# A graph layer on one core: edge loads after the first thirteen move from SyncE's queue to GpSimd's

## The chip, the cores and the metric

The kernel runs on one core of one Trainium2 chip. The metric is the device time of one execution in microseconds, with fp32 data throughout. A core has five engines with a queue of instructions each: TensorE (matrix products), VectorE (called DVE in the profile), ScalarE (ACT), GpSimd (POOL) and SyncE (SP). Any of SP, ACT and POOL can issue DMA transfers; all transfers of the core run on its 16 DMA engines.

## What is computed

The reference is one layer of a graph network, cut here to what matters:

```python
h   = relu(layernorm(x))                       # x: 12500 x 128
agg = segment_sum(edge_attr_48, dst, 12500)    # edge_attr: 412500 x 48, dst sorted
u   = graph_globals[0]                         # 64 numbers, the same for all nodes
hid = relu(concat([h, agg, u]) @ W1 + b1)      # W1: 240 x 256
out = x + (hid @ W2 + b2)                      # W2: 256 x 128
```

Each edge's 48 features are added into the row of its destination node; `dst` is sorted, so neighbouring edges go to neighbouring nodes. Then comes a small two-layer perceptron for each node. The edges are 79 MB of the 95 MB that are moved.

## The kernel before, in words

**The sum over edges as matrix products.** Edges are cut into 403 chunks of 1024 (128 partitions x 8). A chunk is split into two halves of the work, `s = 0` (chunks 0 to 200) and `s = 1` (201 to 402), that go through the kernel side by side. Six chunks make a group; there are 34 groups in each half. For a group, VectorE builds a one-hot matrix (`onehot`, L317): for every edge, 44 columns that compare its shifted destination with 0 to 43. TensorE multiplies the edge features with it (`contract`, L327) and gathers 48 x 199 sums in PSUM. `add` (L343) adds these into `aggT` at the column where the group begins.

**The loop.** The order is written out by hand (the scheduler takes the program's order). The main loop (L647) makes 207 steps; step `CG*i + k` contracts chunk `k` of group `i` of both halves. The rest of the work is placed at steps: a planner dictionary (`at_step`) for dst blocks, `next_x` for loads of x, `next_part` for the layer norm, and a list `pieces` for the perceptron with costs and a credit per step (L666 to 669).

**Edge tiles.** An edge tile `e` holds two chunks, so one load is 384 KB, 128 partitions by two rows of 1536 B. The pool has `PF = 13` buffers. `e_loads` lists the loads in the order in which chunks are used. `next_edges` (L164) takes the next one, allocates a tile and calls `load_edges` (L142). Thirteen are called before the loop (L249); after that each call comes from `contract` (L333), when the last chunk of a tile has been multiplied. The load then has to wait until TensorE has really finished with the buffer.

**Queues.** Before the change SyncE issues: three small loads of `first`, all edge loads (L146), the loads of dst blocks 1 and later (L175, L179; block 1 after the seventh edge load, L252), and all stores of the output (L536, after `ot` has been computed by VectorE, L533). ScalarE issues the loads of x (L211) and dst block 0. GpSimd issues the eight loads of weights (L287 to 294), after its memsets; in the loop it has only two memsets, `mid` (L642) and the pad of the last, short edge tile (L150), whose two remaining loads (L151, L154) are SyncE's.

**The start.** dst block 0 covers two groups, block 1 the next nine. For each block, `shift_dst` (L372) subtracts the base, `spread` transposes it on TensorE (L393) and copies it to `rel`, from which the one-hots are built.

**The perceptron.** For each block of 512 nodes: layer norm (L465, L451, L461), transposes (L477), first layer (L495 for h, L506 for agg, L514 for the relu), second layer (L525) and the sum with x (L533).

Of the kernel before, what the change touches and what calls it, by code (L numbers as in the profile page):

```python
# [21 lines left out]
def kernel(  # L22
# [30 lines left out]
    nc = tc.nc  # L53
# [17 lines left out]
    NFULL = E // CE  # L71
# [67 lines left out]
    bad = const.tile([1, 1], I32)  # L139


    def load_edges(e, c0, n):  # L142

        f = min(n, NFULL - c0)
        if f:
            nc.sync.dma_start(  # L146
                e[:, :f], edge_attr[c0 * CE:(c0 + f) * CE].rearrange("(c p t) d -> p c (t d)", p=P, t=T))
        if f < n:
            last = TAIL // T
            nc.gpsimd.memset(e[:, f], 0.0)  # L150
            nc.sync.dma_start(  # L151
                e[:last, f], edge_attr[NFULL * CE:NFULL * CE + last * T].rearrange("(p t) d -> p (t d)", t=T))
            if TAIL % T:
                nc.sync.dma_start(  # L154
                    e[last:last + 1, f, :(TAIL % T) * DE],
                    edge_attr[None, NFULL * CE + last * T:E].rearrange("a t d -> a (t d)"))

    edges, hots, rels = {}, {}, {}

    e_loads = sorted(  # L160
# [3 lines left out]
    def next_edges():  # L164
        if e_loads:
            _, s, c, n = e_loads.pop(0)
            e = ep.tile([P, CL, T * DE], F32, name="e")
            load_edges(e, c, n)
            for k in range(n):
                edges[c + k] = (e[:, k], k == n - 1)  # L170

    def load_chunks(di, at, c, n, queue):

        full = max(0, min(n, NFULL - c))
        queue.dma_start(di[at:at + full], dst[c * CE:(c + full) * CE].rearrange("(c e) -> c e", e=CE))  # L175
        if full < n:
            for q in range(0, CE, TAIL):
                m = min(TAIL, CE - q)
                queue.dma_start(di[at + full:at + n, q:q + m], dst[None, E - m:E])  # L179
# [57 lines left out]
    with nc.allow_non_contiguous_dma(reason="a few hundred numbers, once"):  # L237
        for s in range(2):
            mid0 = C0[s] * CE
            n = min(NI, (E - mid0) // GE)  # L240
# [8 lines left out]
    for i in range(PF):  # L249
        next_edges()  # L250
        if i == 6:
            dis[1] = load_dst(1, nc.sync)  # L252
# [40 lines left out]
        nc.gpsimd.dma_start(w2, W2.rearrange("(a p) d -> p a d", p=P))  # L293
        nc.gpsimd.dma_start(b2_sb, b2[None, :].to_broadcast([P, D]))

    step = -4
    for k in range(XBUFS):
        load_x(k)
    warm = const.tile([P, 1], F32)
# [20 lines left out]
    def contract(i, k):  # L320

        ps = acc[i % len(acc)]
        o = OFF[k] - OFF[0]
        groups = [(s, s * NI + i, C0[s] + i * CG + k) for s in range(2) if k < chunks[s * NI + i]]
        for t in range(T):
            for s, g, c in groups:
                nc.tensor.matmul(  # L327
                    ps[s * HI:s * HI + DE, o:o + W], edges[c][0][:, t * DE:(t + 1) * DE],
                    hots[g][:, k * T + t, :], start=(k == 0 and t == 0),
                    stop=(k == chunks[g] - 1 and t == T - 1), skip_group_check=True)  # L330
        for s, g, c in groups:
            if edges.pop(c)[1]:
                next_edges()  # L333
# [55 lines left out]
    def turn_dst(df, rows, t0, pool, name):  # L389
        dv = df.rearrange("c (p t) -> c t p", t=T)  # L390
        pt = pool.tile([P, T // 2, P], F32, name=name)
        for t in range(T // 2):
            nc.tensor.transpose(pt[:, t, :rows], dv[:rows, t0 + t, :], ident[:rows, :rows])  # L393
        return pt[:, :, :rows]
# [284 lines left out]
    with tc.If(isbad >= 1):  # L679
        with tc.tile_pool(name="any", bufs=1) as ap:  # L680
            lo_row = ap.tile([1, P], I32, name="lo_row")
            hi_row = ap.tile([1, P], I32, name="hi_row")
            iota_a = ap.tile([P, WA], F32, name="iota_a")
            nc.gpsimd.iota(iota_a, pattern=[[1, WA]], base=0, channel_multiplier=0,
                           allow_small_or_imprecise_dtypes=True)
            nc.gpsimd.memset(aggT, 0.0)

            def windows(s, e_view, r_view, c):
                low_s, high_s = (0, END - 1) if s == 0 else (END, N - 1)
                lo, hi = [nc.values_load(row[0:1, c], min_val=low_s, max_val=high_s,  # L690
                                         skip_runtime_bounds_check_because="clamped on the chip")
                          for row in (lo_row, hi_row)]
                r = ap.tile([P, T], F32, name="r")
                nc.vector.tensor_scalar(r, r_view, float(WA), None, OP.add)
                with tc.For_i(lo, hi + 1, WA) as at:
                    at = nc.s_assert_within(at, low_s, high_s, skip_runtime_bounds_check_because="at most hi")
                    nc.vector.tensor_scalar(r, r, float(-WA), None, OP.add)
                    oh = ap.tile([P, T, WA], F32, name="oh2")
                    nc.vector.tensor_tensor(oh, iota_a[:, None, :].to_broadcast([P, T, WA]),
                                            r[:, :, None].to_broadcast([P, T, WA]), OP.is_equal)  # L700
                    h = slice(s * HI, s * HI + DE)
                    ps = acc[0][h, :WA]
                    for t in range(T):
                        nc.tensor.matmul(ps, e_view[:, t * DE:(t + 1) * DE], oh[:, t, :],
                                         start=(t == 0), stop=(t == T - 1))
                    to = aggT[h, ds(at + shift[s], WA)]
                    nc.vector.tensor_tensor(to, to, ps, OP.add)


            for s, (low_s, high_s) in enumerate(((0, END - 1), (END, N - 1))):  # L710
                for c0 in range(0, NCH, GB):
                    rows = min(GB, NCH - c0)
                    di = dp.tile([P, CE], I32, name="di", bufs=2)
                    load_chunks(di, 0, c0, rows, nc.sync)
                    df = dp.tile([P, CE], F32, name="df", bufs=2)
                    nc.vector.tensor_copy(df[:rows], di[:rows])
                    ends = ap.tile([P, 2], F32, name="ends")
                    nc.vector.tensor_reduce(ends[:rows, 0:1], df[:rows], AX.X, OP.min)
                    nc.vector.tensor_reduce(ends[:rows, 1:2], df[:rows], AX.X, OP.max)

                    nc.vector.tensor_scalar(ends[:rows], ends[:rows], float(low_s), float(high_s), OP.max, OP.min)
                    nc.vector.tensor_scalar(df[:rows], df[:rows], ends[:rows, 0:1], None, OP.subtract)
                    for q, row in ((0, lo_row), (1, hi_row)):
                        pr = pst.tile([1, P], F32, name="pt")
                        nc.tensor.transpose(pr[:, :rows], ends[:rows, q:q + 1], ident[:rows, :rows])
                        nc.vector.tensor_copy(row[:, :rows], pr[:, :rows])
                    rel = ap.tile([P, P, T], F32, name="rel")
                    for t0 in (0, T // 2):
                        nc.scalar.copy(rel[:, :rows, t0:t0 + T // 2].rearrange("p c t -> p t c"),
                                       turn_dst(df, rows, t0, pst, "pt"))  # L730
                    full = min(rows, NFULL - c0)
                    with tc.For_i(0, full, 1) as c:
                        e = ap.tile([P, T * DE], F32, name="e2")
                        nc.sync.dma_start(
                            e, edge_attr[ds(c * CE + c0 * CE, CE)].rearrange("(p t) d -> p (t d)", t=T))
                        windows(s, e, rel[:, ds(c, 1), :].rearrange("p c t -> p (c t)"), ds(c, 1))
                    if full < rows:
                        e = ap.tile([P, 1, T * DE], F32, name="e3")
                        load_edges(e, NFULL, 1)
                        windows(s, e[:, 0], rel[:, full, :], slice(full, full + 1))  # L740
        for s in range(2):
            copy_middle(s)
# [45 lines left out]
```

## Time and profile before

| what | us |
|---|---|
| median of 3 runs (lowest, highest) | 345.6 (343.14, 347.08) |
| the profiled execution's own time | 343.35 |
| its span in the trace | 341.6 |
| TensorE busy (matmuls) in it | 303.0 |
| VectorE busy | 253.5 |
| ScalarE busy | 110.6 |
| GpSimd busy | 13.1 |

The granted clock of TensorE was 0.975 over the span. DMA moved 95.35 MB, 279 GB/s on average. In the rows of the profile, PE is a matmul, PEld a weight load, and a name with q (SPq) the queue of the engine itself; "x <- y: a, b, c" in a table of waits is a us in total, b times, c us the longest. A row of a timeline has the start, the duration, the engine, the line, the operation and its tiles.

### The profile page before, as it was taken

The numbers are of one execution on the slowest core, as the hardware profiler recorded it, in microseconds if no ns is written. First come the engines' busy times: TensorE is split into PE (matmuls) and PEld (weight loads), VectorE is DVE, ScalarE is ACT, GpSimd is POOL, SyncE is SP. The second block draws the span as 40 slices with busy tenths as digits, with TensorE's granted clock in tenths as the row PEclk, the third lists the DMA queues.
The fourth block names the chain that finished last, engine by engine and source line by source line (L and its number), as shares of the span: only waits on it lengthen the run. The fifth ranks groups of instructions, "written<-read, shape, count | busy, mean of one in ns | idle before, by whom it ended". The sixth has DMA issues, their size and how long they took to land.

```text
span 341.6 us, 17111 instructions
## 1 busy us (share of the span) xinstructions
PE 303.0 (89%) x7787; PEld 241.3 (71%) x7788; DVE 253.5 (74%) x413; ACT 110.6 (32%) x238; POOL 13.1 (4%) x44
## 2 busy tenths in 40 slices
PE   1756887999999999889999999889999999999991
PEld 1745764886886786677797696677796796886561
DVE  3768888699896888758878789778899499872320
ACT  3011751805243240333251451233441441251220
POOL 9500000000000000000000000000000000000000
PEclk9969899999999999989999999999999999999998
DMA  5999999999998999998999888989999999920110
GB/s 164 316 356 373 371 372 317 280 347 313 341 289 285 318 300 301 313 310 277 297 335 309 280 300 280 382 266 347 311 304 324 311 296 318 310 97 3 65 63 23
DMA packets 62812, 95.35 MB, mean 279 GB/s; under 512 B 4385, under 2 KB 55949, under 8 KB 62730
## 3 DMA queue, kind: packets, MB, share of 16 engines
q1 hardware_dynamic: 58864, 87.17, 77.1%
q10 hardware_dynamic: 3578, 6.50, 5.7%
q8 instruction: 63, 1.03, 1.3%
q0 software_dynamic: 288, 0.49, 0.5%
q14 instruction: 19, 0.16, 0.1%
HBM read 87.74 MB, written 6.40 MB: 276 GB/s over the span
## 4 chain that ended last, share of the span: by engine, by line
PE 77%; DVE 10%; issue 4%; DMA 4%; SPq 2%; ACT 1%; DVEq 0%; ACTq 0%
PE ps L327 39%; PE po L525 14%; PE ph L495 12%; PE ph L506 7%; DVE oh L317 5%; PE pt L477 4%; DMA di<-in_dst_dram 4%; DVE st L465 1%; PE pt L393 1%; SPq L146 1%; DVE aggT L343 1%; ACT hid L514 1%; ACT xn L461 0%; SPq L241 0%; ACT sc L451 0%
## 5 line engine op out<-in xcount | busy, mean ns | idle before, releaser
L327 PEld LDWEIGHTS ps<-oh,e 128*48 128x48 f32 x6448 | 174.9, 128 | 56.5 <-issue 48.0
L327 PE MATMUL ps<-oh,e 128*48 128x44 f32 x6448 | 183.3, 220 | 8.2 <-issue 4.8
L317 DVE TENSOR_TENSOR oh<-iota,rel 128x2112 f32<-128x2112 f32 (+2 forms) x72 | 157.3, 2205 | 3.8 <-ACT rel L385 2.9
L525 PE MATMUL po<-w,hid 128*64 128x128 f32 (+1 forms) x784 | 59.7, 281 | 3.1 <-issue 2.3
L514 ACT ACTIVATE hid<-ph,bias 128x512 f32<-128x512 f32 (+1 forms) x50 | 31.1, 673 | 85.0 <-PE ph L506 80.9
L495 PE MATMUL ph<-hT,w1h 128*64 128x512 f32 (+1 forms) x200 | 51.9, 597 | 2.5 <-ACT hid L514 2.5
L343 DVE TENSOR_TENSOR aggT<-aggT,ps 48x199 f32 (+1 forms) x68 | 24.3, 357 | 38.8 <-PE ps L327 21.3
L525 PEld LDWEIGHTS po<-w,hid 128*64 128x64 f32 (+1 forms) x784 | 44.4, 139 | 5.9 <-issue 4.2
L461 ACT ACTIVATE xn<-xt,sh,sc 128x128 f32<-128x128 f32 (+1 forms) x100 | 40.6, 484 | 1.7 <-DVE sh L455 1.4
L533 DVE TENSOR_TENSOR ot<-po,xb 128x512 f32<-128x512 f32 (+1 forms) x25 | 17.3, 691 | 18.1 <-PE po L525 17.7
L480 ACT COPY hT<-pt 128x512 f32<-128x512 f32 (+1 forms) x25 | 14.3, 574 | 48.5 <-PE pt L477 48.3
L506 PE MATMUL ph<-aggT,w1a 48*64 48x512 f32 x192 | 26.5, 615 | 0.0
L477 PE MATMUL pt<-ident,xn 128*128 128x128 f32 (+1 forms) x100 | 18.1, 293 | 6.3 <-issue 3.2
L465 DVE BATCH_NORM_STATS2 st<-xt 128x6 f32<-128x128 f32 (+1 forms) x100 | 22.8, 279 | 0.0
L451 ACT ACTIVATE sc<-va,eps 128x8 f32<-128x8 f32 (+1 forms) x13 | 3.9, 301 | 47.2 <-DVE va L450 47.0
L477 PEld LDWEIGHTS pt<-ident,xn 128*128 128x128 f32 (+1 forms) x100 | 10.8, 142 | 10.2 <-issue 3.8
L491 DVE TENSOR_TENSOR xb<-xt,b_sb 128x512 f32<-128x512 f32 (+1 forms) x25 | 16.3, 682 | 0.0
L495 PEld LDWEIGHTS ph<-hT,w1h 128*64 128x64 f32 x200 | 11.1, 137 | 5.1 <-ACT hid L514 3.5
L385 ACT COPY rel<-pt 128x216 f32<-128x216 f32 (+2 forms) x9 | 4.3, 478 | 28.6 <-PE pt L393 28.6
L393 PE MATMUL pt<-ident,df 108*128 108x108 f32 (+2 forms) x36 | 6.3, 302 | 7.2 <-DVE df L372 7.2
L401 ACT ACTIVATE far<-df,bounds 108x1024 f32<-108x1024 f32 (+2 forms) x10 | 11.5, 1145 | 0.2
L150 POOL MEMSET e<- 128x384 f32 x1 | 0.4, 423 | 284.8 <-PE ps L327 284.8
(77 smaller groups left out, 68.3 us busy)
## 6 DMA issues: line engine op xcount, KB each, us to landing
e<-in_edge_attr_dram SPq DMA_DIRECT2D x200, 384.0 KB
xt<-in_x_dram ACTq DMA_DIRECT2D x24, 256.0 KB
out_dram<-ot SPq DMA_DIRECT2D x24, 256.0 KB
di<-in_dst_dram SPq DMA_DIRECT2D x6, 216.0 KB
e<-in_edge_attr_dram SPq DMA_DIRECT2D x2, 192.0 KB
di<-in_dst_dram SPq DMA_DIRECT2D x2, 108.0 KB
e<-in_edge_attr_dram SPq DMA_DIRECT2D x1, 159.0 KB
w1h<-in_L_gnn_W_dram POOLq DMA_DIRECT2D x1, 128.0 KB, 6.8
```

Source lines behind the costliest of these rows:

```text
L317: nc.vector.tensor_tensor(hots[g][:, k0 * T:(k0 + n) * T], iota[:, None, :].to_broadcast([P, n * T, W]), r[:, :, None].to_broadcast([P, n ...
L327: nc.tensor.matmul(ps[s * HI:s * HI + DE, o:o + W], edges[c][0][:, t * DE:(t + 1) * DE], hots[g][:, k * T + t, :], start=(k == 0 and t == ...
L343: nc.vector.tensor_tensor(to, to, acc[i % len(acc)][h, :wg], OP.add)
L461: nc.scalar.activation(xns[j][:m, r], xs[j][:m, r], AF.Relu, bias=sh[:m, c:c + 1], scale=sc[:m, c:c + 1])
L465: parts.append((k, None, lambda i=i, j=j, r=r: nc.vector.bn_stats(st[:m, i * R + r, :], xs[j][:m, r, :])))
L477: nc.tensor.transpose(pt[:, r, :m], xn[:m, r], ident[:m, :m])
L491: nc.vector.tensor_tensor(xb[:m], xs[j][:m], b2_sb[:m, None, :].to_broadcast([m, R, D]), OP.add)
L495: nc.tensor.matmul(phs[j, a][c:c + HI, :R * m], w1h[:, a * P + c:a * P + c + HI], hTs[j][:, :R * m], start=True, stop=False, skip_group_ch ...
L506: nc.tensor.matmul(phs[j, a][c:c + HI], w1a[h, a * P + c:a * P + c + HI], aggT[h, at:at + BN], start=False, stop=True, skip_group_check=True)
L514: nc.scalar.activation(hids[j][:, a, :, :m], phs.pop((j, a))[:, :R * m].rearrange("h (p r) -> h r p", r=R), AF.Relu, bias=bias[:, a:a + 1])
L525: nc.tensor.matmul(pos[j][c:k, r], hids[j][:, a, r, c:k], w2[:, a], start=(a == 0), stop=(a == NH - 1), skip_group_check=True)
L533: nc.vector.tensor_tensor(ot[:m], pos.pop(j)[:m], xbs.pop(j)[:m], OP.add)
```

## The change

`load_edges` and so `next_edges` name the queue that issues the main part of a load. It is SyncE while `step` is below 0, which holds for the thirteen loads before the loop, and GpSimd after that. For this `step = -4` is set further up. The loads of the short last tile stay with SyncE, and so does the edge load of a branch that is not taken with these inputs (L739).

```diff
-    def load_edges(e, c0, n):
+    def load_edges(e, c0, n, queue):
 
         f = min(n, NFULL - c0)
         if f:
-            nc.sync.dma_start(
+            queue.dma_start(
                 e[:, :f], edge_attr[c0 * CE:(c0 + f) * CE].rearrange("(c p t) d -> p c (t d)", p=P, t=T))
...
+    step = -4
     edges, hots, rels = {}, {}, {}
...
             e = ep.tile([P, CL, T * DE], F32, name="e")
-            load_edges(e, c, n)
+            load_edges(e, c, n, nc.sync if step < 0 else nc.gpsimd)
...
-    step = -4
     for k in range(XBUFS):
         load_x(k)
...
-                        load_edges(e, NFULL, 1)
+                        load_edges(e, NFULL, 1, nc.sync)
```

## The prediction

> **What bounds the kernel now.** I read the page first, then the chain of waits, then the two tables of waits (the engines' and SyncE's own queue), then the stretches around the first 40 us and around the gaps of TensorE, and last GpSimd's timeline.
>
> ```profile
> span 341.6 us, 17111 instructions
> PE 303.0 (89%) x7787; PEld 241.3 (71%) x7788; DVE 253.5 (74%) x413; ACT 110.6 (32%) x238; POOL 13.1 (4%) x44
> ...
> q8 instruction: 63, 1.03, 1.3%
> ...
> PE 77%; DVE 10%; issue 4%; DMA 4%; SPq 2%; ACT 1%; DVEq 0%; ACTq 0%
> ```
>
> TensorE is the bound: 303.0 of 341.6 us busy and 77% of the chain. DVE (10%) and one DMA (4%) own the chain only at the start. GpSimd is empty: 13.1 us, nearly all before 13.4 us. Keep the q8 row in mind: 1.03 MB in 63 packets is 16 KB each, and TensorE's 15,575 instructions over 63 are 247 per packet. So TensorE's own program comes in over the same DMA engines as the edges.
>
> In the engines' waits there is one row in which anybody waits for an edge load; below it are the three rows of TensorE alone between 60 and 300 us:
>
> ```profile
> PEld ps L327 <- DMA e<-in_edge_attr_dram: 2.4, 5, 0.8
> ...
> PE ps L327 <- issue: 3.7, 9, 1.0
> PE pt L477 <- issue: 3.2, 2, 1.7
> PE po L525 <- issue: 2.3, 3, 1.6
> ```
>
> Edges cost TensorE 2.4 us in the whole kernel, 1.0 of it before 60 us. The 9.2 us of "issue" (14 gaps) are larger. The long ones on the chain are at 102.61, 138.15, 148.45, 218.29 and 224.32 us (0.73 + 1.02 + 1.69 + 1.52 + 1.61 = 6.57 us); between 136 and 140 us the DMA view reads 379 GB/s against 279 over the span. My reading is that an instruction block arrived late because the engines were full.
>
> SyncE's queue shows why edges are not late:
>
> ```profile
> SPq L146 <- PE ps L327: 135.6, 143, 2.6
> SPq L536 <- DVE ot L533: 48.2, 17, 13.1
> SPq L146 <- DMA e<-in_edge_attr_dram: 22.0, 19, 2.8
> ```
>
> An edge load (L146) waits for TensorE to give a buffer back, in 143 of its waits. So loading runs a full ring of 13 buffers ahead. 202 loads go out from 3.0 to 297.0 us, 1.46 us apart, and 13 of them are 19 us of reserve. The stores (L536) hold the queue up only for 15.2 us between 60 and 300 us, 3.2 at most, well inside that reserve; the rest of the 48.2 comes when no load is left.
>
> **The change part by part.**
>
> *Issue on SyncE falls away:* 189 loads (202 less 13) by the 0.368 us median of L146 are 70 us of a queue nobody waits for. Worth 0.
>
> *Issue on GpSimd is added.* The rows nearest to it:
>
> ```profile
> 7.33 4.89 DVE L317 TENSOR_TENSOR oh<-iota,rel 128x704 f32<-128x704 f32 x6
> ...
> 11.81 0.76 POOL L293 DMA_DIRECT2D w<-in_L_gnn_W_dram  x1
> 12.55 0.56 POOL L294 DMA_DIRECT2D b_sb<-in_L_gnn_b_dram  x1
> 13.08 0.32 POOL L642 MEMSET mid<- 128x212 f32 x1
> ...
> 298.20 0.42 POOL L150 MEMSET e<- 128x384 f32 x1 [284.81 <-PE ps L327]
> ```
>
> The W2 load has the pattern of an edge load (128 partitions by two rows), so I take its 0.76 us: 189 x 0.76 = 144 us, against the 282 us from 15 to 297 (1.49 us per load). GpSimd is half full and keeps up. What hides this is the 19 us of reserve. Without it, a load would be late by 0.76 - 0.37 = 0.39 us each time (189 x 0.39 = 74 us). Value 0; the bounds are 0 and that 74, and 0 is near because the L146 waits say that the reserve is whole.
>
> *A rule that speaks against it.* The Trainium skill, page "SBUF — State Buffer", section "SBUF: two separate sides", says that for a DMA issued by GpSimd its own cores write the descriptors, through a port pair shared with VectorE; a VectorE operation that holds both ports keeps them out until it ends. Taken at its worst, GpSimd issues nothing during the one-hots (L317, 157.3 us, some 147 of them after 15 us): 144 + 147 = 291 us in a window of 282, a kernel 9 us longer. The trace argues against the worst: six one-hots ran back to back from 7.33 to 12.22 us (0.815 us each) while six of GpSimd's eight DMA issues ran at 0.5 to 0.8 us inside the same stretch; neither had a gap. The same section also counts an operation with two SBUF inputs, which the one-hot is, as in the way only of a GpSimd operation that reads SBUF. I go by the row: 0.
>
> *What is queued behind a waiting GpSimd load:* more edge loads, the memset of `mid` (moves from 13 us to behind the loads of the first twelve steps; first read when 28 of 34 groups are done), and the memset of L150, for which SyncE's two tail loads wait (298.7 us, used by TensorE at 313). No one near the chain. SyncE keeps stores and dst loads, which no longer stand behind edge loads; the only wait for one of them is the 5.0 us of L372 for dst block 1, issued with the first thirteen.
>
> *The start changes.* Today load 14 goes out at 20.8 us, since SyncE sends seven loads, then mostly one each time an older one has landed. GpSimd is not behind these: it is free at 13.4 us, and if it too keeps eight in flight, its first edge load waits for its first weight load to land (8.33 + 6.8 = 15.1 us). Five buffers are free by 15.42 us (TensorE has done five steps), so up to five loads of 384 KB start some 5 us earlier. Nobody waits for them. They share engines with this transfer, which is on the chain:
>
> ```profile
> 7.11 12.49 DMA di<-in_dst_dram
> ```
>
> dst block 1 lands at 19.60 us; DVE waits for it, then the one-hots, then TensorE (idle from 15.42 to 21.00). With another ring beside it from about 16 us, its last 2.6 us (my estimate, from its landing less a microsecond) stretch by at most 3072/4096 of themselves, if edges come in packets of two rows: +2.0. But weights and x already share it until about then: bounds 0 and +2.0, I take +0.7. From 20 to 57 us DVE sets the pace, so nothing gives this back.
>
> *Edge waits:* the 1.4 us after 60 us may vanish, as loads no longer stand behind a store. Bounds 0 and -2.4; I take -1.4.
>
> *Instruction blocks.* The second rule: page "DMA: Bandwidth & Descriptors", section "Queues, rings and completion order", says that an engine takes turns between rings packet by packet. By it a block of instructions waits for about one edge packet; if GpSimd's packets hold two rows, that is 3072 B instead of 1536, at 23 B/ns per engine (375 GB/s over 16) 0.07 us more, 63 x 0.07 = +4 us if nothing hides it. The trace disagrees with the rule's picture of a short wait: the first weight load (128 KB, 8 KB per engine) took 6.8 us to land behind seven edge loads. A newcomer waits for a backlog, whichever ring holds it; then the change is worth nothing here. Bounds -6.6 (the five gaps go) and +4; I go by the row, 0.
>
> *Sum:* -1.4 + 0.7 + 0 = -0.7 us on the profiled execution's 343.35 us (341.6 span and 1.75 around it) gives 342.65. The median of the runs, 345.6, lies 2.25 above that execution, so 344.9 on the median.
>
> **Rivals.**
>
> (A) *The transfer is hidden anyway*, the forecast: 344.9, its own range 342.2 to 348.5. For it: 143 waits for buffers, 19 us of reserve. Chance 0.40.
>
> (B) *GpSimd becomes the bound.* One mechanism, in the loop of loads: if an issue there costs over 1.49 us instead of 0.76, loads fall behind TensorE and the reserve drains. At 291 us of GpSimd time it is +9, so 355. Against it: the overlapped rows above. For it: the trace has only eight such issues, none with a wait in front. Chance 0.14. An off-shoot: the DMA engines are slower on GpSimd's rings. The need is about 310 GB/s and 375 were reached, so over 17% worse would decide; 360 and more, 0.04.
>
> (C) *Contention at the start and at instruction blocks:* +2.0 for dst and +4 for blocks, with no gain: 351.6. For it: PE gaps already coincide with full engines, and x loads on ACT and edges would both be free to run earlier. Chance 0.15.
>
> (D) *The block gaps close*, because loads leave one by one as buffers come free and not in bursts after a blocked queue: -1.4 and -6.6 + 0.7 is -7.3, so 338.3 at best; half of the gaps give 341.6. For it: the gaps fall where the engines are full. Against: TensorE itself frees buffers in bursts. Chance 0.27.
>
> (E) *It does not do what it says:* from GpSimd the loads could still come no earlier, since buffers decide. That is part of A.
>
> **How the numbers follow.** 1% is 3.5 us, about what a measurement of this kernel can tell from no change. A is "within 1%": 0.40. B with its off-shoot and C are slower: 0.33. D is faster: 0.27. The range holds A, D down to 339 and C and B up to 355, leaving out the slow off-shoot and the ends of B and D.
>
> **What would show it.** Right: L146 as a POOL row of about 0.76 us, its waits mostly for PE; PE's "issue" rows still near 9 us; L372's wait for dst near 5 to 7 us; "PEld ps <- DMA e" under 2.4. B: that row at tens of us and POOL's issues above 1.4 us. C: dst landing after 21 us, more and longer issue gaps. D: the five gaps gone and TensorE's busy share above 90%. The forecast falls if loads from GpSimd land much later than a free buffer, or if TensorE's instruction blocks react to whose ring the edges are in.

## The result, and the profile after

| | median us | lowest, highest | ratio to before [95%] |
|---|---|---|---|
| before, beside it | 346.34 | 343.14, 347.48 | 1 |
| changed kernel | 360.66 | 357.85, 364.57 | 1.0402 [1.0281, 1.0522] |
| before, on another chip | 349.18 | 345.83, 351.25 | 1 |
| changed kernel, on that chip (`a2_after`) | 357.69 | 355.78, 360.88 | 1.0239 [1.0186, 1.0292] |

The change costs 2.4 to 4.0%. The forecast was no change (344.9, in a range up to 355). The profiled execution after took 357.85 us, 14.5 more than the one before (343.35). Medians are of all runs; ratios are of the fast ones alone, those within 1.5% of the fastest of their kernel ("none" where there was only one).

The page after: span, busy times, queues, chain, and two groups (busy us and mean ns of one; idle us before them and who ended it).

```profile
span 356.1 us, 17111 instructions
...
PE 308.6 (87%) x7787; PEld 246.3 (69%) x7788; DVE 253.7 (71%) x413; ACT 110.9 (31%) x238; POOL 147.6 (41%) x233
...
q0 software_dynamic: 21408, 74.63, 64.0%
q1 hardware_dynamic: 7584, 13.03, 10.9%
...
PE 76%; DMA 9%; DVE 6%; issue 5%; SPq 1%; ACT 1%; DVEq 0%; ACTq 0%
...
L146 POOL DMA_DIRECT2D e<-in_edge_attr_dram x189 | 134.4, 712 | 164.6 <-PE ps L327 159.1
L317 DVE TENSOR_TENSOR oh<-iota,rel 128x2112 f32<-128x2112 f32 (+2 forms) x72 | 157.4, 2205 | 4.0 <-ACT rel L385 3.2
```

GpSimd issues a load in 0.71 us and for 159.1 of its 164.6 idle us waits for TensorE to free a buffer: it is not the bound. A one-hot of VectorE takes 2205 ns, as before. DMA now has 9% of the chain, against 4%, and almost all of it lies in two pieces (chain in order of time: start, us, what):

```profile
5.93 13.45 DMA e<-in_edge_attr_dram
19.81 17.73 DMA e<-in_edge_attr_dram
```

Both are edge loads of **SyncE**. The first is the seventh; SyncE waited for it to land before it issued the eleventh. The second is the twelfth of the first thirteen, issued at 19.81 us. TensorE needed it, and it landed at 37.54. The engines' waits, then the issues in the whole kernel, then those from 7.5 to 20.6 us alone (last number: median us from issue to landing):

```profile
PEld ps L327 <- DMA e<-in_edge_attr_dram: 14.6, 22, 2.9
PE ps L327 <- DMA e<-in_edge_attr_dram: 7.2, 4, 2.8
...
DVE df L372 <- DMA di<-in_dst_dram: 3.7, 1, 3.7
```
```profile
e<-in_edge_attr_dram POOLq DMA_DIRECT2D x188, 384.0 KB, 5.4
```
```profile
e<-in_edge_attr_dram SPq DMA_DIRECT2D x6, 384.0 KB, 18.8
e<-in_edge_attr_dram POOLq DMA_DIRECT2D x5, 384.0 KB, 9.1
```

Waits for edges were 2.4 us and are 21.8 (14.6 + 7.2). Before 45 us they are 15.0 (7.8 and 7.2). Most of the rest is a label: each of GpSimd's loads landed at least 9 us before the first product that used it. GpSimd's first five edge loads, issued from 15.94 to 19.73 us, took 9.1 us in the median. SyncE's last six were issued from 8.02 to 20.32 us; the trace gives the landing of only one of them, the thirteenth tile, and the 18.8 is that one (39.12 us). By the packets on SyncE's ring the thirteen tiles were complete at 25.2 us before and at 38.2 after. So tiles 14 to 18 were there first, and TensorE waited for tiles 9 to 12 and took the thirteenth as it landed. What the engines carried from 20 to 36 us says why (packets, MB, share of 16 engines), before and then after:

```profile
DMA packets 4006, 5.98 MB, mean 374 GB/s; under 512 B 261, under 2 KB 3620, under 8 KB 4004
...
q1 hardware_dynamic: 3572, 5.16, 91.9%
```
```profile
DMA packets 2472, 5.85 MB, mean 366 GB/s; under 512 B 252, under 2 KB 1365, under 8 KB 2469
...
q0 software_dynamic: 983, 3.47, 59.1%
q1 hardware_dynamic: 1053, 1.55, 28.0%
```

The bytes are nearly the same; their order is not. q1 is SyncE's ring, q0 GpSimd's (a ring is the list of transfers that one queue has handed to the DMA engines). The two rings took about as many turns (983 and 1053 packets), but most of GpSimd's packets hold three rows of 1536 B (15,072 packets of 4608 B in the kernel), SyncE's one. So the loads that were due got 1.55 MB and those that were not got 3.47. TensorE's timeline shows the price (start, us, matmuls, then the idle time before); the last row is from the kernel before:

```profile
25.07 1.51 PE L327 MATMUL ps<-oh,e 128*48 128x44 f32 x30 [0.36 <-DMA e<-in_edge_attr_dram]
28.52 1.67 PE L327 MATMUL ps<-oh,e 128*48 128x44 f32 x34 [1.94 <-DMA e<-in_edge_attr_dram]
32.96 1.51 PE L327 MATMUL ps<-oh,e 128*48 128x44 f32 x30 [2.77 <-DMA e<-in_edge_attr_dram]
...
37.58 4.37 PE L327 MATMUL ps<-oh,e 128*48 128x44 f32 x96 [2.17 <-DMA e<-in_edge_attr_dram]
```
```profile
40.51 2.36 PE L327 MATMUL ps<-oh,e 128*48 128x44 f32 x96
```

96 matmuls took 4.37 us, where 96 had taken 2.36. Two stretches have the reason (busy us and count of each engine, the granted clock, then the DMA engines' share and GB/s), after and then before:

```profile
20.00:30.00 10.00, 7.70 (x138) 6.78 (x136) 9.10 (x24) 1.91 (x4) 2.58 (x4) 0.50 1.04 374
30.00:40.00 10.00, 5.06 (x94) 4.67 (x92) 2.43 (x9) 5.86 (x13) 2.02 (x3) 0.50 0.95 300
```
```profile
20.00:30.00 10.00, 7.91 (x201) 7.30 (x203) 9.33 (x24) 1.92 (x4) 0.00 (x0) 0.78 1.06 375
30.00:40.00 10.00, 6.83 (x178) 5.65 (x173) 8.62 (x17) 6.33 (x14) 0.00 (x0) 0.83 1.07 371
```

The late edges did not start this. In both kernels the granted clock fell to 0.50 while TensorE stood still before its first use of dst block 1, at 17.6 us before and at 18.9 after. Before, it was 1.00 again from 24.4 to 34.6 us; after, it stayed at 0.50 up to 42.8. In `a2_after`, the same program as after, it was 1.00 from 25.3 to 32.1 us, and TensorE was late by nearly as much (8.8 us against 9.6 in the table below). So the low clock adds little to the delay.

To separate the start from the rest, I took the start time of the n-th matmul of L327 in each trace less that in the trace before (where they begin at 30.8, 45.9, 83.2 and 314.2 us). One execution each:

| kernel | GpSimd issues | lag at 385th | 641st | 1451st | last |
|---|---|---|---|---|---|
| `b_again`, the kernel before | none | -0.5 | -1.1 | 1.6 | 9.5 |
| after | all from 14th | 9.6 | 6.5 | 9.3 | 14.6 |
| `a2_after` | the same | 8.8 | 5.6 | 6.3 | 17.5 |
| `e2_early` | steps 0 to 39 | 8.1 | 4.9 | 6.1 | 6.7 |
| `e8_early2` | the same | 7.5 | 4.4 | 4.4 | 10.0 |
| `e4_wait` | all, held at the start | 2.6 | 0.3 | 5.8 | 11.3 |
| `e5_late2` | from step 40 | 0.4 | -0.3 | 0.4 | 8.6 |
| `e7_late3` | the same | 0.5 | 0.1 | 0.1 | 2.9 |
| `t1_rows` | none, longer rows | -0.8 | -0.3 | -0.2 | -0.4 |

After is 9.6 us behind at 31 us, gets 3.1 of it back while the kernel before is held up by VectorE, and then loses another 8.1 slowly up to the end. That looks like two losses, but they are not equally well seen. `b_again` is the kernel before, traced a second time in a longer execution (353.01 us): it has no lag at the start, and 9.5 us at the last matmul. So the first two columns tell kernels apart; the last one, from one execution each, does not.

### The profile page after: what moved, and what is told of

It is laid out like the page before. It is cut to its first block, busy times and chain, and to the rows that moved or that the text cites. A ratio compares the mean times of both kernels' runs of the same rounds, so it can differ in the third digit from the quotient of the medians.

```text
span 356.1 us, 17111 instructions
## 1 busy us (share of the span) xinstructions
PE 308.6 (87%) x7787; PEld 246.3 (69%) x7788; DVE 253.7 (71%) x413; ACT 110.9 (31%) x238; POOL 147.6 (41%) x233
## 3 DMA queue, kind: packets, MB, share of 16 engines
q8 instruction: 63, 1.03, 1.2%
## 4 chain that ended last, share of the span: by engine, by line
PE 76%; DMA 9%; DVE 6%; issue 5%; SPq 1%; ACT 1%; DVEq 0%; ACTq 0%
PE ps L327 39%; PE po L525 13%; PE ph L495 12%; DMA e<-in_edge_attr_dram 9%; PE ph L506 7%; PE pt L477 4%; DVE oh L317 3%; PE pt L393 1%; SPq L146 1%; DVE st L465 1%; DVE aggT L343 1%; ACT hid L514 1%; ACT xn L461 0%; SPq L242 0%; ACT sc L451 0%
## 5 line engine op out<-in xcount | busy, mean ns | idle before, releaser
L327 PEld LDWEIGHTS ps<-oh,e 128*48 128x48 f32 x6448 | 179.9, 129 | 73.7 <-issue 55.0
L327 PE MATMUL ps<-oh,e 128*48 128x44 f32 x6448 | 189.2, 221 | 23.6 <-issue 14.2
L146 POOL DMA_DIRECT2D e<-in_edge_attr_dram x189 | 134.4, 712 | 164.6 <-PE ps L327 159.1
L317 DVE TENSOR_TENSOR oh<-iota,rel 128x2112 f32<-128x2112 f32 (+2 forms) x72 | 157.4, 2205 | 4.0 <-ACT rel L385 3.2
L525 PE MATMUL po<-w,hid 128*64 128x128 f32 (+1 forms) x784 | 57.9, 278 | 1.9 <-issue 1.2
L495 PE MATMUL ph<-hT,w1h 128*64 128x512 f32 (+1 forms) x200 | 53.3, 605 | 1.8 <-ACT hid L514 1.8
L525 PEld LDWEIGHTS po<-w,hid 128*64 128x64 f32 (+1 forms) x784 | 43.2, 137 | 4.5 <-issue 2.7
L495 PEld LDWEIGHTS ph<-hT,w1h 128*64 128x64 f32 x200 | 11.6, 138 | 4.3 <-ACT hid L514 2.8
L385 ACT COPY rel<-pt 128x216 f32<-128x216 f32 (+2 forms) x9 | 4.3, 479 | 29.1 <-PE pt L393 25.3
## 6 DMA issues: line engine op xcount, KB each, us to landing
e<-in_edge_attr_dram SPq DMA_DIRECT2D x12, 384.0 KB, 18.8
```

The costliest lines, as they stand in the source:

```text
L146: queue.dma_start(e[:, :f], edge_attr[c0 * CE:(c0 + f) * CE].rearrange("(c p t) d -> p c (t d)", p=P, t=T))
L317: nc.vector.tensor_tensor(hots[g][:, k0 * T:(k0 + n) * T], iota[:, None, :].to_broadcast([P, n * T, W]), r[:, :, None].to_broadcast([P, n ...
L327: nc.tensor.matmul(ps[s * HI:s * HI + DE, o:o + W], edges[c][0][:, t * DE:(t + 1) * DE], hots[g][:, k * T + t, :], start=(k == 0 and t == ...
L495: nc.tensor.matmul(phs[j, a][c:c + HI, :R * m], w1h[:, a * P + c:a * P + c + HI], hTs[j][:, :R * m], start=True, stop=False, skip_group_ch ...
L525: nc.tensor.matmul(pos[j][c:k, r], hids[j][:, a, r, c:k], w2[:, a], start=(a == 0), stop=(a == NH - 1), skip_group_check=True)
```

## The experiments

**1. The start alone, and the rest alone.** Theory: the loss is made at the start. Rival: it is made all along by GpSimd's loads.

```diff
 e1_late, e5_late2, e7_late3:
-            load_edges(e, c, n, nc.sync if step < 0 else nc.gpsimd)
+            load_edges(e, c, n, nc.sync if step < 40 else nc.gpsimd)
 e2_early, e8_early2:
+            load_edges(e, c, n, nc.gpsimd if 0 <= step < 40 else nc.sync)
 e3_five:
+            load_edges(e, c, n, nc.gpsimd if 0 <= step < 5 else nc.sync)
```

> Edge loads go to GpSimd only from step 40 on, some 75 us into the kernel; until then all are SyncE's. Overtaking theory (the loads from GpSimd take the DMA engines away from the thirteen loads of SyncE that TensorE needs first; 10 of the 14 us are lost before 90 us): the start is as before, TensorE waits for edges under 2 us before 60 us, 347 to 351 us. Rival, the ring of GpSimd is worse all along (descriptors written by GpSimd, larger packets, instruction blocks of TensorE late): most of the loss stays, 355 us or more, and TensorE's issue gaps after 90 us stay near 15 us.

> GpSimd issues the edge loads of steps 0 to 39 only, SyncE all later ones. Overtaking theory: nearly the whole loss of the start is there, 354 to 358 us, with SyncE's loads 8 to 13 landing near 38 us and TensorE waiting over 10 us for edges before 45 us. Rival, a worse ring all along: a fifth of the loads is moved, so a fifth of the loss, 348 to 350 us.

> GpSimd issues only the five loads of steps 0 to 4 (1.9 MB, some 5 us of the DMA engines at 370 GB/s), SyncE the rest. Overtaking theory: SyncE's last of the first thirteen are late by at most these 5 us, and nothing follows, as the next loads stand behind them in SyncE's queue: 348 to 352 us. Rival, a worse ring all along: 5 of 189 loads, no difference, 346 to 347 us.

> The same program as the late switch, with more runs. If the ring of GpSimd costs TensorE time in the steady part (later instruction blocks), 351 to 355 us against some 347 of the kernel before, with 12 us or more of TensorE's issue gaps; if only the start counts, within 2 us of the kernel before.

> The late switch (GpSimd from step 40 on, 256 rows of 1536 B per load) once more, on the same chip as the two below. If the steady part costs what the earlier ten runs say, 1.010 to 1.015 of the kernel before; if these were chance, within 0.5%.

> GpSimd for steps 0 to 39 only, with more runs. If the start is the whole cost, the same as the changed kernel of this call within 1%. If the steady part costs a percent of its own, 1% to 2% below it: 1.02 to 1.03 of the kernel before.

| kernel | median us | before beside it | ratio to before [95%] |
|---|---|---|---|
| `e2_early` | 355.24 | 347.82 | 1.0231 [1.0113, 1.0349] |
| `e8_early2`, the same | 353.34 | 349.18 | 1.0125 [1.007, 1.018] |
| `e3_five` | 350.7 | 347.82 | 1.0001 [0.9959, 1.0042] |
| `e1_late` | 354.12 | 347.82 | none |
| `e5_late2`, the same | 352.21 | 347.89 | 1.0106 [1.0047, 1.0166] |
| `e7_late3`, the same | 350.29 | 348.28 | 1.002 [0.997, 1.007] |

The start alone costs 1.3 to 2.3%, and its trace has the mark of the start, the lag of 4.4 to 4.9 us at the 641st matmul. Waits of `e2_early`:

```profile
PEld ps L327 <- DMA e<-in_edge_attr_dram: 11.3, 10, 3.3
...
PE ps L327 <- DMA e<-in_edge_attr_dram: 8.2, 4, 3.2
```

Five loads alone (`e3_five`) lag by 4.8 us at the 385th matmul and 1.9 at the 641st, and the ratio shows no loss, though the median of all its runs lies 2.9 us above that of the kernel before: inconclusive. The late switch has no start lag, and its ratios say between nothing and 1%; alone it didn't settle whether the rest costs anything. The best sign of a second loss is another pair, on one chip: six runs of `e8_early2` took 351.03 to 354.47 us, six of `a2_after`, in which GpSimd goes on to the end, 355.78 to 360.88. The medians are 4.4 us apart.

**2. The same loads on GpSimd, but not before SyncE's have landed.** GpSimd copies one number out of the thirteenth tile ahead of its first edge load. If sharing at the start is the cause, the lag goes; if GpSimd's issuing itself is, it stays.

```diff
+            if len(firsts) == PF:
+                nc.gpsimd.tensor_copy(landed, firsts[-1][0:1, 0, 0:1])
+            firsts.append(e)
             load_edges(e, c, n, nc.sync if step < 0 else nc.gpsimd)
```

> As the changed kernel, but GpSimd copies one number out of the thirteenth edge tile before its first edge load, so it can't start until that load has landed (near 25 us). Overtaking theory: the start is nearly that of the kernel before, as the later loads have a reserve: 346 to 352 us. Rival, a worse ring all along: 357 to 361 us, as in the changed kernel. Second rival, loads from GpSimd come too late at all: slower than the changed kernel, over 362 us.

> The changed kernel with GpSimd's first edge load held until the thirteenth tile has landed, with more runs. If overtaking at the start is the whole cost, 0.997 to 1.006 of the kernel before; if the steady part costs a percent, 1.008 to 1.018.

`e4_wait` 353.39 us, 1.0106 [1.002, 1.0193]; `e9_wait2` 356.62, 1.0115 [1.0019, 1.021]. The wait in `e4_wait`, and the landing of SyncE's thirteenth tile (again the only one of its full tiles that the row's time holds):

```profile
POOL landed L172 <- DMA e<-in_edge_attr_dram: 14.6, 1, 14.6
```
```profile
e<-in_edge_attr_dram SPq DMA_DIRECT2D x12, 384.0 KB, 9.6
```

GpSimd stood still for 14.6 us and its first edge load went out at 29.71 instead of 15.94 us; the thirteenth tile then landed in 9.6 instead of 18.8 us. The lag at the 641st matmul is 0.3 (-0.9 in `e9_wait2`), as in the kernels whose start is SyncE's. Loads that begin **later** take the lag away: the loss at the start is shown to be the sharing. The gain in time is less well shown: `e9_wait2` has a ratio from two of its six runs, and the median of all six lies only 1.1 us below that of `a2_after` on the same chip. What remains, 1.1% in both ratios, would be the second loss.

**3. Is it the size of the packets?** A row of 3072 B (two chunk rows that lie next to each other in memory) makes SyncE's packets twice as long, and GpSimd's 6144 B instead of 4608. The sums are then over other edges; the work is the same. In `t2_sp_rows` the edit holds where `queue is nc.sync`, in the last three of the table where `queue is nc.gpsimd`.

```diff
-                e[:, :f], edge_attr[c0 * CE:(c0 + f) * CE].rearrange("(c p t) d -> p c (t d)", p=P, t=T))
+                e[:, :f].rearrange("p c f -> p (c f)"),
+                edge_attr[c0 * CE:(c0 + f) * CE].rearrange("(p t) d -> p (t d)", p=P))
```

> The kernel before, all on SyncE's queue, but each partition takes sixteen edges in a row per load: 128 rows of 3072 B in place of 256 of 1536 B, the same bytes (the sums are then over other edges than the reference's). If TensorE's instruction blocks wait longer behind larger packets, the issue gaps grow to 11 us or more and the time by 2 to 4 us, with no GpSimd in it. If it is not the size but the second ring, no change: within 1 us of the kernel before.

> The changed kernel, but SyncE's first thirteen edge loads take sixteen edges in a row per partition: rows and packets of 3072 B in place of 1536 B (their sums are then over other edges). If the engines take turns between the rings packet by packet, SyncE's ring gets about twice the share against GpSimd's packets of 4608 B: its last loads land near 30 us in place of 38, the lag at 28 us falls from 9.5 to 4 to 6 us, and the time by 3 to 5 us, to 353 to 357. Rival, what counts is that GpSimd's loads are ahead in a common queue, whatever the packets: no change, 358 to 361.

> The changed kernel, but the edge loads of GpSimd take sixteen edges in a row per partition: rows of 3072 B, so packets of at least that and perhaps 6144 B against SyncE's 1536 B (their sums are over other edges). Turns packet by packet: with packets of 6144 B SyncE's ring gets a smaller share yet, the lag at 28 us grows by 2 to 4 us, 361 to 365; with packets of 3072 B it shrinks, 355 to 358. Rival, a common queue: no change, 358 to 361.

> The late switch (GpSimd from step 40 on), with GpSimd's rows of 3072 B (sums over other edges). If the cost of the steady part is that TensorE's instruction blocks wait for GpSimd's larger packets, it moves with the size of these: about 355 us for 6144 B, 350 for 3072 B, against 352 in the late switch. If not, 351 to 353 as there.

> The late switch with 128 rows of 3072 B per load of GpSimd (sums over other edges), once more, same chip. If the cost goes with the number of descriptors that GpSimd writes and not with the size of its packets, 0.997 to 1.003 as before, a percent below the late switch of this call; if the first result was chance, 1.010 or more.

| kernel | rows of 3072 B | median us | before beside it | ratio to before [95%] |
|---|---|---|---|---|
| `t1_rows` (else as before) | all, SyncE | 347.0 | 347.89 | 1.0015 [0.9976, 1.0053] |
| `t2_sp_rows` (else as after) | SyncE's first 13 | 358.25 | 348.1 | none |
| `t3_pool_rows` (else as after) | GpSimd's | 353.92 | 348.1 | 1.0153 [1.0071, 1.0236] |
| `t4_late_rows` (GpSimd from step 40) | GpSimd's | 349.39 | 348.1 | 0.9987 [0.9944, 1.003] |
| `t8_late_rows2`, the same | GpSimd's | 349.48 | 348.28 | 1.0114 [1.0073, 1.0155] |

Longer packets by themselves do nothing (`t1_rows`). At the start they move the moment at which SyncE's thirteen tiles are complete: 38.2 us in after, 34.5 in `t2_sp_rows`, 39.9 in `t3_pool_rows` (last packet of these tiles). The lag at the 641st matmul goes with it: 6.5, 3.8 and 7.8 us. From 20 to 36 us, `t2_sp_rows` and then `t3_pool_rows`:

```profile
q0 software_dynamic: 881, 3.15, 57.2%
q1 hardware_dynamic: 644, 1.81, 31.5%
```
```profile
q0 software_dynamic: 647, 3.20, 55.6%
q1 hardware_dynamic: 1086, 1.78, 33.3%
```

The direction is that of turns packet by packet; the sizes are not. Equal turns would give GpSimd 1.5 times SyncE's bytes in `t2_sp_rows` (4608 to 3072 B) and 4 times in `t3_pool_rows` (6144 to 1536 B); the rows give 1.7 and 1.8, with 647 packets beside 1086 in the second. (q1 also holds loads of dst blocks, 0.26 and 0.36 MB of its bytes here and 0.05 in after.) So "one packet each" holds only roughly. Nor did the times of whole runs follow: 353 to 357 us were expected of the first and 361 to 365 of the second, and the medians are 358.25 and 353.92. That is unexplained. For the second loss, fewer and longer packets gave 0.9987 once and 1.0114 once, with medians that hardly differ: that idea is not supported.

**4. Is it that GpSimd is busy?** SyncE issues every load; GpSimd clears each tile before its load from step 40 on, so each load also waits for that clear.

```diff
+            if step >= 40:
+                nc.gpsimd.memset(e, 0.0)
+            load_edges(e, c, n, nc.sync)
```

> The kernel before with all edge loads on SyncE's queue, but from step 40 on GpSimd clears each tile (some 0.65 us) when it comes free, ahead of its load, so that it writes to the tiles' memory as often as in the late switch and issues no transfer. If GpSimd's being busy is what costs TensorE time, 1.010 or more; if it is the descriptors of its transfers, 0.997 to 1.004.

`m1_busy` 351.46 us, 1.0173 [1.0109, 1.0238]. GpSimd was busy with it for 110.4 us, against 134.4 with the loads of the changed kernel:

```profile
L170 POOL MEMSET e<- 128x768 f32 x150 | 110.4, 738 | 178.2 <-PE ps L329 109.7
```

Its median (348.28 for the kernel before beside it) speaks for a cost of GpSimd's activity; but its profiled execution took 346.51 us, 3.2 above the one before, and lags by 3.1 at the last matmul. Unclear.

**5. How well is the kernel before known, and is its own start a wait that could be moved?** `b_again` is the kernel before, unchanged. `f1_dst` sends dst block 1 behind the second edge load instead of the seventh (`if i == 1:`).

> The kernel before itself, once more, for the spread of its profile: both theories expect a ratio of 1.00 to the kernel before. TensorE's issue gaps between 60 and 300 us were 9.2 us in the first profile; if they come out near 9 again, the 12 to 15 of the kernels in which GpSimd issues are due to GpSimd, and if they come out at 12 or more, they are the spread of this kernel.

> The kernel before with dst block 1 issued behind the second edge load instead of the seventh. If what is queued first on the ring sets the start, dst block 1 lands some 5 us earlier (near 14 us in place of 19.6), VectorE's wait for it goes from 5.0 us to under 1, and the kernel gains 3 to 5 us: 342 to 344. Rival: the edge tiles that stand behind it come later by as much and TensorE waits for them instead, no gain.

> The changed kernel itself, with more runs, on the same chip as the two below: both theories expect 1.03 to 1.05 of the kernel before, 358 to 364 us.

`b_again` 348.52 us, 1.0047 [1.0002, 1.0093]: the same program differs by half a per cent, so nothing below that is read here. Its trace has 14.3 us of TensorE's issue gaps, above the 12 that its expectation named as the spread of this kernel. `f1_dst` 346.67 us, 0.9978 [0.9944, 1.0012]. Its `shift_dst` begins at 15.50 instead of 19.72 us, but TensorE now waits for edges instead, 12.3 us where it was 2.4:

```profile
PEld ps L327 <- DMA e<-in_edge_attr_dram: 7.1, 7, 3.5
PE ps L327 <- DMA e<-in_edge_attr_dram: 5.2, 3, 3.4
```

Between 20 and 40 us the DMA engines of the kernel before are full (1.06 and 1.07 in the stretches above), so here the order of transfers only chose who waits. The gain of 3 to 5 us that was expected did not come, and no version here beats the kernel before. `a2_after`, expected at 1.03 to 1.05, gave 1.024: the size of the loss is no better known than 2.4 to 4.0%.

## Why the prediction was wrong

- **The step that failed** is "The start changes", at its sentence "Nobody waits for them. They share engines with this transfer". True of the five early loads, but the list of victims was wrong. Only dst block 1 was priced (+0.7); it came earlier than before (`shift_dst` at 18.42 instead of 19.72 us). SyncE's own loads of tiles 8 to 13 were on the same engines, undelivered, and due before tile 14. They were complete 11 to 13 us later (35.9 to 38.2 for 25.2 us) and cost 7.5 to 9.6 us by the 385th matmul, of which 4.4 to 6.5 were still there at the 641st (four traces). The text even said that SyncE sends its last tiles "one each time an older one has landed" up to 20.8 us, and that loads from GpSimd's ring would start at 15.1: the two together are the answer.
- **The rule on turns** (the Trainium skill, "DMA: Bandwidth & Descriptors", "Queues, rings and completion order": an engine changes rings after each packet) was applied to dst block 1 and to instruction blocks, and for the blocks set aside. It was not applied to edges against edges, where it mattered: 983 packets beside 1053 agree with it; 647 beside 1086 in `t3_pool_rows` don't agree with strict turns. Two rows per packet were assumed where there were three.
- **Edge waits:** -1.4 forecast. Instead +19.4 us of waits in the table, 15.0 of them real and before 45 us. The reserve of 13 buffers, rightly read for the steady part, doesn't exist at the start, when it is still being filled.
- **Issue on GpSimd** was right: 0.71 us each for 0.76, first edge load at 15.94 for 15.1, 134 us hidden, waits nearly all for buffers. Rival B did not happen, and the port rule's worst (+9) did not either: 2205 ns for the one-hot in both kernels.
- **Instruction blocks** were taken as 0 between -6.6 and +4, and stay open. TensorE's "issue" gaps between 60 and 300 us, 9.2 us before, are 14.8 in the changed kernel:

```profile
PE ps L327 <- issue: 12.9, 15, 2.4
PE po L525 <- issue: 1.2, 2, 0.7
...
PE pt L477 <- issue: 0.7, 1, 0.7
```

  But `b_again`, the kernel before unchanged, has 14.3. In all eight traces with SyncE issuing there (before, `b_again`, `e2_early`, `e8_early2`, `e3_five`, `t1_rows`, `f1_dst`, `m1_busy`) the gaps are 9.2 to 15.4 us, mean 12.1; in all eleven with GpSimd, 11.6 to 18.2, mean 15.0. The means are 3 us apart, two traces of one program 5. So whether GpSimd's loads lengthen the gaps is not shown, and the place of the second loss is open. The gaps themselves are waits for TensorE's own program, as the prediction read them: in every kernel, each one over 0.6 us ends 1.2 to 1.6 us after a 16 KB packet of the instruction queue has landed.
- **Rival C** had the right word, contention, with the wrong victim and too small a size: 6.0 us over the median before (351.6), where 8.5 (357.69 to 349.18) and 14.3 (360.66 to 346.34) were measured.

## What to carry to other kernels

One queue for many loads is also an order of priority. When part of it goes to a second queue, list what is still undelivered in the first at that moment: the newcomers get a share of the engines ahead of older loads that are needed sooner. Hold the second queue until the first has landed its backlog, or switch once the reserve is full; by their ratios both cost less here than the plain switch, and neither beat one queue. Of the 9.6 us lost at the start, 3.1 were won back.

## What was not expected of the hardware

- A load issued by GpSimd goes in packets of three 1536 B rows (4608 B, 224.5 ns in the mean) where SyncE's are of one (74.0 ns). Per byte that is the same, 20.5 and 20.8 B per ns on an engine; it changed shares, not throughput (366 GB/s from 20 to 36 us, for 374 before).
- TensorE's granted clock stayed at 0.50 from 18.9 to 42.8 us in one trace of the changed kernel, and 96 matmuls then took 2.0 us longer; in another trace of the same program it was 1.00 for 6.8 us in between.
- TensorE has 9 to 18 us of issue gaps between 60 and 300 us in every version, the longer ones while it waits for its own instructions; a second trace of an unchanged program had 5 us more of them.
